# Layer 1's q and k by seven products over pairs of rows, normalised on ScalarE, with the order of four engines written out

## The chip, the cores and the metric

The kernel runs on one core of one Trainium2 chip. A core has five engines that run their own instruction queues and meet at semaphores: PE (TensorE, with a weight load, PEld, that overlaps the product before it), DVE (VectorE), ACT (ScalarE), POOL (GpSimd) and SP (SyncE, which here only issues DMAs). The metric is the device time of one execution in microseconds.

## The reference

`x` is 128 rows of 256 tokens with 256 channels. Two layers of attention follow, each with a group norm ahead of it and its input added back. All is float32.

```python
x = x + L0(gn(x))        # gated attention in each row, 8 heads of 32, a bias added after softmax
x = x + L1(gn(x))        # banded attention in each row, 4 heads of 64

def L1(x):                                   # x2: (128 rows, 256 tokens, 256 channels)
    q, k, v = split(x2 @ w_in.T + b_in, 3)
    scores = q @ k.T / sqrt(64), -inf where |i - j| > 16
    return softmax(scores) @ v @ w_out.T + b_out
```

The group norm of a layer needs the mean and variance over all rows, so layer 1 starts when layer 0 has ended. The bias of k adds the same number to all scores of one query, which softmax takes out again.

## The kernel before, and where the change touches it

A row is kept as [128 partitions, 2 halves, 256 tokens], channels on the partitions. A product of a [128x128] weight quarter with [128x256] of a row is two PE instructions, since the data are float32; a projection of 256 to 256 channels is four such products a row.

Layer 0 (lines 552 to 817) already computes its q, k, v and gate by seven products for eight. Two rows and two halves form a 2x2 block matrix `x[:, 0..3]`; POOL makes four sums of them (`sum_rows`, L584 to L587, tile `ts`), `sum_weights` (L158) has made the sums of the weight quarters once, `Seven.product` (L604) issues the seven products into a PSUM bank and a shared one, `Seven.take` (L619) copies what stands in the bank to SBUF on ACT between products, and `Seven.add` (L629) adds the copies together on POOL. `stretch` (L749) interleaves two weights (q with k, v with gate) and, between the late products, the four output products of an earlier row. In layer 0 the order of PE, ACT and DVE is the program's order (`manual_schedule`, L786).

Layer 1 (L826 on) has no such order: the tile framework's scheduler places its instructions. Its loop takes two rows a turn. For each row:

- `piece(s, 0)` (L836) normalises a row on DVE (`normalized`, L493: subtract the mean, multiply by rstd, two instructions of 128x256), and loads a pair of rows ahead (`load1`, L548, on SP).
- `piece(s, 1)` and `piece(s, 2)` make q and k by `by_channel` (L513, four products each) and copy them to SBUF on ACT, adding the bias (L849, two instructions each).
- `piece(s, 3)` makes v by 32 small products (L857) and copies it on ACT (L864).
- `scores` (L867) makes the band of the scores in blocks of 64 keys (L878), takes the exponential on ACT (L886), multiplies by the mask on POOL (`1p`, L888) and folds two halves together on POOL (`1zp`, L895).
- `attend` (L898) makes the weighted sum (L910) and the softmax's denominator (L920) in one pair of PSUM banks.
- `divide` (L927) copies the denominator on ACT (`1z`, L933), inverts it on DVE (`1rz`, L935), multiplies on DVE (`1at`, L937) and keeps its least value (`zmin`, L939).
- `project` (L941) is the output projection (four products, `1po`, L513), and `finish` (L945) adds bias and input (`1ot`, L956), transposes back (L960), both on DVE, and SP stores.

PSUM has eight banks. In layer 1 four are a ring (`psum(lay, "1", 4, 0)`, L827) that the scores, the projections and v all draw from in the order of issue; the other four are two pairs for `attend`.

A turn of the loop, for the rows s and s+1, issues: scores of s, s+1; attend of s-2, s-1; project of s-4, s-3; q and k of s+2, s+3; v of s+2, s+3; normalising of s+4, s+5; finish of s-4, s-3; divide of s-2, s-1.

Of the kernel before, what the change touches and what calls it, by code (L numbers as in the profile page):

```python
# [9 lines left out]
F32 = mybir.dt.float32  # L10
# [29 lines left out]
def conv_preact_kernel(  # L40
# [112 lines left out]
    sums = {w: const.tile([P, len(NS), P], F32, name=f"sums_{w}") for w in "qkvg"}  # L153

    def quarter(w, kt, m):
        source, col = (gate_sb, 0) if w == "g" else (qkv_sb, "qkv".index(w) * C)
        return source[:, kt, col + m * P : col + (m + 1) * P]

    def sum_weights():
        for w in "qkvg":  # L160
            s1, s2, s3, s4, n11 = (sums[w][:, n, :] for n in range(len(NS)))
            w00, w10, w01, w11 = (quarter(w, kt, m) for m in range(2) for kt in range(2))
            nc.gpsimd.tensor_tensor(s1, w01, w11, ALU.add)
            nc.gpsimd.tensor_tensor(s2, s1, w00, ALU.subtract)
            nc.gpsimd.tensor_tensor(s3, w00, w01, ALU.subtract)
            nc.gpsimd.tensor_tensor(s4, w10, s2, ALU.subtract)
            nc.gpsimd.tensor_scalar(n11, w11, -1.0, None, op0=ALU.mult)

    def stationary(w, n):

        if n <= 2:
            return quarter(w, n - 1, 0)
        return sums[w][:, NS.index({3: "s4", 4: "n11", 5: "s1", 6: "s2", 7: "s3"}[n]), :]
# [164 lines left out]
    with ExitStack() as early:  # L338
# [121 lines left out]
        for m in range(NM):  # L460
# [17 lines left out]
            if m == NM // 4:  # L478
                load_weights()
                sum_weights()  # L480
# [48 lines left out]

    x1 = dram.tile([S, 2, P, R], F32, name="x1")  # L530
# [8 lines left out]
    with ExitStack() as both:  # L539
        st1 = both.enter_context(tc.tile_pool(name="st1", bufs=1))  # L540
        stats1 = st1.tile([P, 2, S // 2, 6], F32, name="stats1")
        big1 = both.enter_context(tc.tile_pool(name="big1", bufs=2))
# [8 lines left out]
        with ExitStack() as lay0:  # L551
# [27 lines left out]
            def sum_rows(i):  # L579

                if 2 * i >= S:
                    return
                x, t = xns[i], row.tile([P, 4, R], F32, tag="ts", name=f"ts{i}", bufs=1)
                nc.gpsimd.tensor_tensor(t[:, 0], x[:, 2], x[:, 0], ALU.subtract)  # L584
                nc.gpsimd.tensor_tensor(t[:, 1], x[:, 3], t[:, 0], ALU.subtract)
                nc.gpsimd.tensor_tensor(t[:, 2], x[:, 3], x[:, 2], ALU.subtract)
                nc.gpsimd.tensor_tensor(t[:, 3], t[:, 1], x[:, 1], ALU.subtract)  # L587
                tss[i] = t

            class Seven:  # L590


                def __init__(self, w, i):
                    self.w, self.i = w, i
                    self.to = row.tile([P, 4, R], F32, tag=w, name=f"{w}{i}")
                    res[w, i] = self.to
                    self.mid = row.tile([P, 2, R], F32, tag="mid", name=f"mid{w}{i}")

                def open(self):
                    self.ps = proj_bank(f"p{self.w}{self.i}")  # L600

                def product(self, n, two=None):
                    x, t = xns[self.i], tss[self.i]
                    moving = {1: x[:, 0], 2: x[:, 1], 3: x[:, 3], 4: t[:, 3], 5: t[:, 0], 6: t[:, 1], 7: t[:, 2]}[n]  # L604
                    out = two if n == 2 else self.ps[:, 1 if n in (3, 5) else 0, :]

                    first = n == 1 or (n == 2 and self.w in "qv")
                    flags = dict(stop=n in (2, 3, 4), skip_group_check=True)
                    if self.w != "v":
                        nc.tensor.matmul(out, lhsT=stationary(self.w, n), rhs=moving, start=first, **flags)  # L610
                        return
                    for t2 in range(2):
                        cols = slice(t2 * P, (t2 + 1) * P)
                        nc.tensor.matmul(  # L614
                            out[:, cols], lhsT=moving[:, cols], rhs=stationary(self.w, n),
                            start=first and t2 == 0, **flags
                        )

                def take(self, what):  # L619
                    if what == "15":  # L620
                        nc.scalar.copy(self.to[:, 0:4:3, :], self.ps)
                    elif what == "6":
                        nc.scalar.copy(self.mid[:, 0, :], self.ps[:, 0, :])
                    elif what == "7":
                        nc.scalar.copy(self.mid[:, 1, :], self.ps[:, 0, :])
                    else:
                        nc.scalar.copy(self.to[:, 1:3, :], self.ps)

                def add(self, two):  # L629
                    nc.gpsimd.tensor_tensor(self.to[:, 0], self.to[:, 0], two, ALU.add)  # L630
                    nc.gpsimd.tensor_tensor(self.to[:, 2:4], self.to[:, 2:4], self.mid, ALU.add)
# [57 lines left out]
            def divide(s, zs):  # L689
# [3 lines left out]
                z = att.tile([P, 2, R], F32, tag="z", name=f"z{s}")  # L693
# [10 lines left out]
            def attend(s):  # L704
# [9 lines left out]
                at = row.tile([P, 2, R], F32, tag="at", name=f"at{s}")  # L714
# [20 lines left out]
            def output(s):  # L735

                if s < 0:
                    return
                st[s]["po"] = proj_bank(f"po{s}")
                for m in range(2):  # L740
                    for kt in range(2):
                        nc.tensor.matmul(  # L742
                            st[s]["po"][:, m, :], lhsT=out_sb[:, kt, m * P : (m + 1) * P],
                            rhs=st[s]["at"][:, kt, :],
                            start=(kt == 0), stop=(kt == 1),
                        )
                        yield

            def stretch(names, i, s):  # L749

                po = output(s)
                if 2 * i >= S:
                    for _ in po:
                        pass
                    return
                f, g = (Seven(w, i) for w in names)


                for p in (f, g):
                    p.open()  # L760
                    p.product(1)
                    p.product(5)
                    p.take("15")
                twos = proj_bank(f"p2{names}{i}")
                two = row.tile([P, 2, R], F32, tag="two", name=f"two{names}{i}")
                f.product(2, twos[:, 0, :])
                g.product(2, twos[:, 1, :])
                nc.scalar.copy(two, twos)  # L768
                for p in (f, g):
                    p.product(3)  # L770
                    p.product(6)
                    p.take("6")

                for n, what in ((7, "7"), (4, "34")):
                    f.product(n)
                    f.take(what)
                    next(po, None)
                    g.product(n)
                    g.take(what)
                for _ in po:  # L780
                    pass
                for n, p in enumerate((f, g)):
                    p.add(two[:, n, :])


            with tc.manual_schedule(engines={mybir.EngineType.PE, mybir.EngineType.Activation, mybir.EngineType.DVE}):  # L786
# [8 lines left out]
                for s in range(S + 1):  # L795
# [14 lines left out]
                    least(s - 1, z)  # L810
                    if s == S - 1:
                        most1 = join_most(st1, stats1, 1)
                        load1(0)
                        load1(1)
# [11 lines left out]
        with ExitStack() as lay:  # L826
# [3 lines left out]
            st, hd, outs = {}, {}, {}  # L830

            weights = [att.tile([P, 2, 2 * WROW], F32, name=f"1p{i}", bufs=1) for i in range(4)]
            for p in weights:
                nc.gpsimd.memset(p, 0.0)

            def piece(s, n):  # L836
                if s >= S:
                    return
                if n == 0:
                    if s % XG == 0:  # L840
                        load1(s // XG + 1)
                    st[s] = {"xn": normalized(row, ygs[s // XG][:, s % XG], mean1, rstd1, f"1_{s}")}
                elif n in (1, 2):
                    w = "qk"[n - 1]
                    ps = by_channel(w_in_t, (n - 1) * C, st[s]["xn"], f"p1{w}{s}")
                    a = row.tile([P, 2, R], F32, tag=w, name=f"1{w}{s}")
                    for half in range(2):
                        b = bqk[:, 2 * (n - 1) + half : 2 * (n - 1) + half + 1]
                        nc.scalar.activation(a[:, half, :], ps[:, half, :], AF.Identity, bias=b)  # L849
                    st[s][w] = a  # L850
                else:
                    xn = st[s]["xn"]
                    ps = proj_bank(f"p1v{s}").rearrange("p a (b c) -> p (a b) c", c=P)
                    for b in range(NB):
                        for kt in range(2):
                            for half in range(2):
                                nc.tensor.matmul(  # L857
# [335 lines left out]
```

## Time and profile before

| | us |
|---|---|
| median of 3 runs (2 of them 3288.93 and 3289.75) | 3289.35 |
| the profiled execution | 3289.14 |
| its span, first to last instruction | 3287.4 |
| PE busy | 3204.8 (97%) |
| DVE busy | 2732.7 (83%) |
| ACT busy | 1820.0 (55%) |
| POOL busy | 1250.6 (38%) |

The costliest groups that belong to layer 1, from the page's list: the reciprocal of the denominator on DVE (L935, 128 x 3342 ns), the products of q and k and of the output projection on PE (L513, 1024 instructions each at about 380 ns, pipelined), v's products (L857), the mask on POOL (L888, 128 x 1822 ns), the copies of q on ACT (L849, 256 x 470 ns), and the normalising on DVE (L493, 256 x 410 ns). A group's line gives: line, engine, operation, output and inputs, sizes, count, busy us, mean ns of one, and the idle time of the engine ahead of it with what ended that. A line of the order of time gives: start us, length us, engine, line, operation, tiles, count, and in brackets the engine's idle time just before and what ended it. Several instructions of one kind that follow each other are merged into one line.

### The profile page before, as it was taken

What the parts mean: (1) busy time and instruction counts of PE and PEld (TensorE: products, weight loads), DVE (VectorE), ACT (ScalarE), POOL (GpSimd) and SP (SyncE); (2) the same over time, 40 slices, a digit from 0 to 9 for tenths busy, and PEclk for the clock granted to TensorE, in tenths of its full rate; (3) what the DMA queues carried; (4) which work ended last, traced back from release to release, by engine and by line L of the source; (5) the groups of instructions that cost most, each with busy time, mean ns of one, the idle gap of its engine ahead of it and who ended that gap; (6) DMA issues with size and microseconds to landing.
All of it is one profiled execution on the core that took longest, in us unless ns stands there. A gap on an engine that the chain in (4) does not pass through costs nothing.

```text
span 3287.4 us, 86502 instructions
## 1 busy us (share of the span) xinstructions
PE 3204.8 (97%) x37193; PEld 2506.1 (76%) x37193; DVE 2732.7 (83%) x3794; ACT 1820.0 (55%) x3866; POOL 1250.6 (38%) x1135
## 2 busy tenths in 40 slices
PE   7799999999999999999999999799999999999997
PEld 4567777777777777777777777588888888888886
DVE  4759999999999999999999999667777777777776
ACT  4566666666666666666666666344444444444442
POOL 3034444444444444444444444133333323333232
PEclk8899999999999999999999999899999999999998
DMA  9931111111111111111111110012222222222221
GB/s 382 411 87 56 49 38 36 40 33 40 34 40 40 33 40 34 40 35 39 34 40 40 33 40 21 20 40 66 54 65 66 53 66 55 64 66 53 66 56 45
DMA packets 346327, 209.35 MB, mean 64 GB/s; under 512 B 273608, under 2 KB 339152, under 8 KB 339664
## 3 DMA queue, kind: packets, MB, share of 16 engines
q1 hardware_dynamic: 345040, 201.37, 21.2%
q8 instruction: 294, 4.82, 0.6%
q0 software_dynamic: 752, 2.36, 0.2%
q14 instruction: 97, 0.79, 0.1%
q10 hardware_dynamic: 144, 0.00, 0.0%
HBM read 136.59 MB, written 67.11 MB: 62 GB/s over the span
## 4 chain that ended last, share of the span: by engine, by line
PE 93%; DMA 3%; DVE 3%; ACT 0%; issue 0%; SPq 0%; DVEq 0%; ACTq 0%
PE sim L640 8%; PE p1v L857 7%; PE av L667 7%; PE 1po L513 7%; PE po L742 7%; PE p1q L513 7%; PE p1k L513 7%; PE bv L667 7%; PE pv L614 6%; PE pq L610 5%; PE pk L610 5%; PE pg L610 5%; PE zs L681 4%; DMA xs<-in_x_dram 3%; PE 1sim L878 3%; PE 1avz L910 2%
## 5 line engine op out<-in xcount | busy, mean ns | idle before, releaser
L651 ACT ACTIVATE ex<-sim 128x512 f32<-128x512 f32 x1024 | 527.4, 601 | 249.7 <-PE sim L640 249.7
L935 DVE RECIPROCAL 1rz<-1z 128x512 f32<-128x512 f32 x128 | 427.8, 3342 | 174.2 <-ACT 1z L933 174.2
L657 DVE TENSOR_TENSOR both<-ex 128x512 f32<-128x512 f32 x512 | 483.7, 984 | 77.8 <-ACT ex L651 77.8
L888 POOL TENSOR_TENSOR 1p<-1ex,seen 128x768 f32<-128x768 f32 x128 | 233.3, 1822 | 736.3 <-ACT 1ex L886 736.3
L697 DVE RECIPROCAL d<-d 128x512 f32<-128x512 f32 x128 | 429.2, 3353 | 4.4
L742 PE MATMUL po<-at,out_sb 128*128 128x256 f32 x1024 | 287.4, 384 | 12.1 <-DVE at L715 12.1
L849 ACT ACTIVATE 1q<-p1q,bqk 128x256 f32<-128x256 f32 x256 | 107.5, 470 | 345.1 <-PE p1q L513 345.1
L640 PE MATMUL sim<-q,k 32*128 32x256 f32 x4096 | 295.7, 401 | 1.1 <-ACT ex L651 1.1
L630 POOL TENSOR_TENSOR v<-v,twovg 128x256 f32<-128x256 f32 x64 | 72.8, 1137 | 551.1 <-ACT twovg L768 551.1
L640 PEld LDWEIGHTS sim<-q,k 32*128 32x128 f32 x4096 | 186.4, 184 | 102.7 <-issue 63.8
L513 PE MATMUL 1po<-1at,w_out_t 128*128 128x256 f32 x1024 | 242.7, 390 | 4.9 <-DVE 1at L937 4.9
L667 PE MATMUL av<-ex,v 128*32 128x256 f32 x4096 | 247.5, 382 | 0.0
L513 PE MATMUL p1q<-xn,w_in_t 128*128 128x256 f32 x1024 | 244.0, 381 | 2.0 <-DVE xn L493 1.1
L667 PE MATMUL bv<-bias_sb,v 128*32 128x256 f32 x4096 | 244.4, 379 | 0.0
L513 PE MATMUL p1k<-xn,w_in_t 128*128 128x256 f32 x1024 | 241.9, 379 | 0.0
L857 PEld LDWEIGHTS p1v<-w_in_t,xn 128*64 128x64 f32 x4096 | 222.2, 137 | 21.6 <-issue 21.6
L857 PE MATMUL p1v<-w_in_t,xn 128*64 128x128 f32 x4096 | 237.9, 274 | 0.0
L513 PEld LDWEIGHTS 1po<-1at,w_out_t 128*128 128x128 f32 x1024 | 191.6, 192 | 55.0 <-ACT 1z L933 23.9
L513 PEld LDWEIGHTS p1q<-xn,w_in_t 128*128 128x128 f32 x1024 | 195.3, 191 | 29.4 <-issue 1.3
L513 PEld LDWEIGHTS p1k<-xn,w_in_t 128*128 128x128 f32 x1024 | 194.7, 190 | 26.5
L742 PEld LDWEIGHTS po<-at,out_sb 128*128 128x128 f32 x1024 | 187.0, 193 | 34.1 <-issue 7.7
L493 DVE TENSOR_SCALAR xn<-yg,mean,rstd 128x256 f32<-128x256 f32 x256 | 93.9, 410 | 138.9 <-PE p1v L857 138.9
(226 smaller groups left out, 6708.1 us busy)
## 6 DMA issues: line engine op xcount, KB each, us to landing
pr<-in_L_conv_pair_repr_dram SPq DMA_DIRECT2D x32, 1024.0 KB, 23.0
x<-o SPq DMA_DIRECT2D x64, 512.0 KB, 2.8
yg<-x SPq DMA_DIRECT2D x64, 512.0 KB, 4.2
out_dram<-1o SPq DMA_DIRECT2D x256, 128.0 KB, 4.0
xg<-in_x_dram SPq DMA_DIRECT2D x252, 128.0 KB, 3.1
xs<-in_x_dram SPq DMA_DIRECT2D x15, 2048.0 KB, 21.7
xs<-in_x_dram SPq DMA_DIRECT2D x2, 1024.0 KB, 17.9
qkv_sb<-in_L_conv_qkv_proj_dram POOLq DMA_DIRECT2D x4, 192.0 KB, 12.6
```

Of the source, the lines that this page charges most:

```text
L513: nc.tensor.matmul(ps[:, m, :], lhsT=w[:, kt, col + m * P : col + (m + 1) * P], rhs=xn[:, kt, :], start=(kt == 0), stop=(kt == 1),)
L610: nc.tensor.matmul(out, lhsT=stationary(self.w, n), rhs=moving, start=first, **flags)
L614: nc.tensor.matmul(out[:, cols], lhsT=moving[:, cols], rhs=stationary(self.w, n), start=first and t2 == 0, **flags)
L640: nc.tensor.matmul(sims[j][:, kt, :], lhsT=k[p0 : p0 + D0, 2 * r + half, kt * P : (kt + 1) * P], rhs=q[p0 : p0 + D0, 2 * r + half, :], sta ...
L651: nc.scalar.activation(ex[:, j], sims[j], AF.Exp, scale=1.0 / math.sqrt(D0))
L657: nc.vector.tensor_tensor(both[:, j : j + 2], ex[:, j : j + 2, 0, :], ex[:, j : j + 2, 1, :], ALU.add)
L667: nc.tensor.matmul(to[D0 * j : D0 * (j + 1), half, :], lhsT=v[:, 2 * r + half, c0 : c0 + D0], rhs=weights(4 * half + j, kt), start=(kt == ...
L697: nc.vector.reciprocal(d, d)
L742: nc.tensor.matmul(st[s]["po"][:, m, :], lhsT=out_sb[:, kt, m * P : (m + 1) * P], rhs=st[s]["at"][:, kt, :], start=(kt == 0), stop=(kt == 1),)
L857: nc.tensor.matmul(ps[KB * half : KB * (half + 1), b, :], lhsT=xn[:, kt, KB * b : KB * (b + 1)], rhs=w_in_t[:, kt, 2 * C + P * half : 2 * ...
L888: nc.gpsimd.tensor_tensor(p.rearrange("p j (r c) -> p (j r) c", c=WROW)[:, :, 0 : 2 * WSTEP] .rearrange("p r (t c) -> p r t c", c=WSTEP)[: ...
L935: nc.vector.reciprocal(rz, z)
```

## The change

The helpers of layer 0 (`Quarters`, `row_sums`, `Seven`, `sevens`, and `one_by_one` for the output products) are lifted out so that both layers use them; layer 0 calls them in the order it had. In layer 0 the tiles `z` and `at` now have one buffer instead of two. The weight sums of layer 1's q and k are made in a new tile for each, by ten small POOL instructions.

Layer 1 is rewritten:

- `normal(i, by_scalar)` normalises a pair of rows in four instructions, the first two pairs on DVE, all others on ACT (`Identity` with scale and bias), and makes the four row sums on POOL.
- `stretch(i, po)` makes q and k of a pair by seven products each. q's bias goes in with three of ACT's copies; k's bias is left out. The four output products of one row stand between the late products.
- `divide` is split into `total`, `inverse`, `divide` and `least`, so that each can be placed.
- PE, ACT, DVE and POOL follow the order of the program.

```diff
+    class Seven:
+        def __init__(self, pool, weights, x, t, name, tag, by_token=False, bias=None):
...
+        def copy(self, to, ps, half):
+            if self.bias is None:
+                nc.scalar.copy(to, ps)
+            else:
+                nc.scalar.activation(to, ps, AF.Identity, bias=self.bias[:, half : half + 1])
+
+        def take(self, what):
+            if what == "15":
+                nc.scalar.copy(self.to[:, 0:4:3, :], self.ps)
+            elif what == "6":
+                self.copy(self.mid[:, 0, :], self.ps[:, 0, :], 0)
+            elif what == "7":
+                self.copy(self.mid[:, 1, :], self.ps[:, 0, :], 1)
+            elif self.bias is None:
+                nc.scalar.copy(self.to[:, 1:3, :], self.ps)
+            else:
+                self.copy(self.to[:, 1, :], self.ps[:, 0, :], 1)
+                nc.scalar.copy(self.to[:, 2, :], self.ps[:, 1, :])
+
+        def add(self, two):
+            nc.gpsimd.tensor_tensor(self.to[:, 0], self.to[:, 0], two, ALU.add)
+            nc.gpsimd.tensor_tensor(self.to[:, 2:4], self.to[:, 2:4], self.mid, ALU.add)
+
+    def sevens(pool, f, g, name, po):
+        for p in (f, g):
+            p.open()
+            p.product(1)
+            p.product(5)
+            p.take("15")
...
+        f.product(2, twos[:, 0, :], first=True)
+        g.product(2, twos[:, 1, :])
+        if f.bias is None:
+            nc.scalar.copy(two, twos)
+        else:
+            f.copy(two[:, 0, :], twos[:, 0, :], 0)
+            g.copy(two[:, 1, :], twos[:, 1, :], 0)
+        for p in (f, g):
+            p.product(3)
+            p.product(6)
+            p.take("6")
+        for n, what in ((7, "7"), (4, "34")):
+            f.product(n)
+            f.take(what)
+            next(po, None)
+            g.product(n)
+            g.take(what)
+        for _ in po:
+            pass
+        for n, p in enumerate((f, g)):
+            p.add(two[:, n, :])
...
-                z = att.tile([P, 2, R], F32, tag="z", name=f"z{s}")
+                z = att.tile([P, 2, R], F32, tag="z", name=f"z{s}", bufs=1)
...
+                        if by_scalar:
+                            nc.scalar.activation(x, y, AF.Identity, bias=shift1[:, col], scale=rstd1[:, col])
+                        else:
+                            nc.vector.tensor_scalar(
+                                x, y, mean1[:, col], rstd1[:, col], op0=ALU.subtract, op1=ALU.mult
+                            )
+                tss[i] = row.tile([P, 4, R], F32, tag="ts", name=f"1ts{i}", bufs=2)
+                row_sums(tss[i], xns[i])
...
+            with tc.manual_schedule(engines={
+                mybir.EngineType.PE, mybir.EngineType.Activation, mybir.EngineType.DVE, mybir.EngineType.Pool
+            }):
+                normal(0, False)
+                values(0)
+                values(1)
+                normal(1, False)
+                nc.vector.scalar_tensor_tensor(shift1, mean1, -1.0, rstd1, op0=ALU.mult, op1=ALU.mult)
+                stretch(0, iter(()))
+                for s in range(0, S + 4, 2):
+                    if s < S:
+                        scores(s)
+                        scores(s + 1)
+                    one, two = (s - 2, s - 1) if s <= S else (-1, -1)
+                    attend(one)
+                    attend(two)
+                    total(one)
+                    total(two)
+                    for _ in project(s - 4):
+                        pass
+                    inverse(one)
+                    finish(s - 4)
+                    divide(one)
+                    inverse(two)
+                    divide(two)
+                    least(one)
+                    least(two)
+                    stretch(s // 2 + 1, project(s - 3))
+                    finish(s - 3)
+                    normal(s // 2 + 2, True)
+                    values(s + 2)
+                    values(s + 3)
```

## The prediction

> **What bounds the kernel now.** I read the slices of the span first, then the chain that ended last, then busy time by stretch, then the order of time inside one turn of layer 1's loop.
>
> ```profile
> PE   7799999999999999999999999799999999999997
> DVE  4759999999999999999999999667777777777776
> ACT  4566666666666666666666666344444444444442
> POOL 3034444444444444444444444133333323333232
> PE 93%; DMA 3%; DVE 3%; ACT 0%; issue 0%; SPq 0%; DVEq 0%; ACTq 0%
> 2360.00:3240.00 880.00, 880.00 (x12571) 777.59 (x12570) 652.33 (x890) 371.49 (x886) 303.05 (x198) 1.00 0.24 60
> ```
>
> The dip of PE in the slices, near 2100 us, parts layer 0 from layer 1. In the last row (PE, PEld, DVE, ACT, POOL, clock) PE works in all of 880 us of layer 1 at full clock, DVE in 74%, ACT in 42%, POOL in 34%. So a product removed from PE is time gained, as long as nothing else comes late. One turn (two rows) in weight loads of PE:
>
> ```profile
> 2799.98 1.37 PEld L878 LDWEIGHTS 1sim<-1q,1k 64*64 64x64 f32 x61 [0.17 <-issue]
> 2803.63 3.32 PEld L513 LDWEIGHTS 1po<-1at,w_out_t 128*128 128x128 f32 x16 [0.39 <-ACT 1z L933]
> 2806.97 1.70 PEld L513 LDWEIGHTS p1q<-xn,w_in_t 128*128 128x128 f32 x8
> 2808.70 1.70 PEld L513 LDWEIGHTS p1k<-xn,w_in_t 128*128 128x128 f32 x8
> 2814.19 3.47 PEld L857 LDWEIGHTS p1v<-w_in_t,xn 128*64 128x64 f32 x64 [0.33 <-issue]
> 2817.83 1.37 PEld L878 LDWEIGHTS 1sim<-1q,1k 64*64 64x64 f32 x61 [0.17 <-issue]
> ```
>
> A turn is 2817.83 - 2799.98 = 17.85 us. From 2157.45 (the scores of rows 4 and 5, the first turn with everything in it) to 3246.19 (the last scores) there are 61 of them. From q to k is 1.73 us for four products of 128x256 (eight instructions, two to an f32 product): 0.4325 us a product.
>
> **What goes.** q and k take 16 products a turn before and 14 after: 2 x 0.4325 = 0.865 us less on PE, which nothing covers. The 32 small products of v, the scores, the attention and the eight output products stay, at their prices.
>
> **What is added, and where it lies.** Layer 0 already runs this scheme, so most rows are at hand. Times below count from a turn's first scores.
>
> *PE waits for ACT inside the stretch.* Products 6, 7 and 4 of one weight go to one bank in turn, and each must first be copied out. Layer 0 shows how tight this is:
>
> ```profile
> 1015.30 0.41 PEld L610 LDWEIGHTS pq<-ts,sums_q 128*128 128x128 f32 x2
> 1016.14 0.37 ACT L623 COPY midq<-pq 128x256 f32<-128x256 f32 x1 [0.27 <-PE pq L610]
> 1016.59 0.41 PEld L610 LDWEIGHTS pq<-ts,sums_q 128*128 128x128 f32 x2
> ```
>
> The copy begins 0.84 us after product 6's load and ends at 1016.51; product 7 loads 0.08 later. Other weight loads go 0.05 us after the copy that they wait for, so 0.03 us is spare. In layer 1 q's copies add a bias. The row for that is L849 (below), 0.470 us, not 0.373. Two round trips of q (6 to 7, 7 to 4) come 0.07 us late each: **+0.14 us** a turn. If the copies were no longer it is 0; if all four round trips, k's too, stalled by the full 0.1 it is 0.4. k's copies carry no bias and have an output product between, so I keep 0.14.
>
> *POOL.* It gets eight instructions a turn: four row sums and two adds (256 and 512 wide) for each of q and k. The scores of the next turn wait for the last add.
>
> ```profile
> L630 POOL TENSOR_TENSOR q<-q,twoqk 128x256 f32<-128x256 f32 x54 | 40.5, 750 | 253.8 <-ACT twoqk L768 253.8
> L630 POOL TENSOR_TENSOR k<-k,twoqk 128x256 f32<-128x256 f32 x54 | 63.3, 1172 | 0.0
> L631 POOL TENSOR_TENSOR q<-q,midq 128x512 f32<-128x512 f32 x55 | 70.0, 1272 | 86.3 <-ACT q L627 86.3
> L631 POOL TENSOR_TENSOR g<-g,midg 128x512 f32<-128x512 f32 x54 | 92.6, 1714 | 0.0
> L849 ACT ACTIVATE 1q<-p1q,bqk 128x256 f32<-128x256 f32 x256 | 107.5, 470 | 345.1 <-PE p1q L513 345.1
> L493 DVE TENSOR_SCALAR xn<-yg,mean,rstd 128x256 f32<-128x256 f32 x256 | 93.9, 410 | 138.9 <-PE p1v L857 138.9
> ```
>
> The same instruction has two prices in layer 0: 0.75 or 1.17 us, 1.27 or 1.71. In the order of time the dear ones lie beside DVE sums of two SBUF tiles (both, d). The Trainium skill's page "SBUF — State Buffer", section "Who interferes with whom", says that a VectorE instruction with two SBUF inputs, or in a two-port mode, contends with GpSimd, and one with a single SBUF input does not. Layer 1's VectorE work after the change (reciprocal, reduce, transposes, and sums with one input in PSUM) is of the free kind, and before the change L895 on POOL takes 1.27 us beside zmin and ot there. So I take the cheap prices; the dear ones are the other end.
>
> Cheap: q's last output leaves ACT at about 12.6 (product 4 of q loads at 10.9, +0.84, then 0.47 + 0.37). POOL then does 1.27 + 0.72 + 1.27 and is done at 15.9; the scores come at 17.1: 1.2 us spare. The four row sums follow (2.8 us, to 18.7), just ahead of the next turn's mask product, which waits for its exponentials until 17.1 + 1.94 = 19.0. POOL's sum is 2 x (1.82 + 1.27) + 4.0 + 3.0 = 13.2 us of 17.1. Cost on the path: 0.
>
> *Normalising moves from DVE to ACT.* The page "ScalarE: Activation LUTs", "Rules for kernel authors", speaks against it: multiply and add belong on VectorE; with its 0.3 us + 0.83 ns an element I estimate 0.51 us for 256 elements, against 0.41 on DVE. The nearest row is L849's 0.470, at a pitch of 0.42. Four are 1.7 us by the row, 2.05 by the page. Either is hidden: ACT sums to about 11.3 us of 17.1 (exponentials 1.6, z 1.6, copies of q and k 5.1, this 1.8, v 1.2). They run from 13.2 to 15.0, and v's copy, queued behind them, is not due until about 15.4. With the page's 0.3 us more v's bank still comes free in time. DVE loses 1.6 us; 12.5 us remain.
>
> *The order by hand.* DVE does: reciprocal, output of row s-4, divide, reciprocal, divide, two reduces, output of row s-3. It starts at 3.5, when z is there. The first output product's bank is read by 8.2, wanted again at 10; the second is read by about 15, wanted at 17.5. SP's order is unchanged: a load of yg waits for the output of the same turn (15.4), takes its 4.2 us and is wanted ten later. Dropping k's bias adds no instruction.
>
> *Layer 0.* Its order on PE, DVE, ACT and SP stays. Tiles z and at get one buffer. z is written at 1008.73 and last read (zmin) by 1004.6; at is written at 1015.41 and last read at about 1005.7: covered by 4 us or more. Ten weight sums (0.45 us each in L163's rows, 4.4 us) stand on POOL ahead of layer 0's first row sum. POOL idles there from 185.7 to 193.99, so 0; 4.4 us once if they are released only at the end of that gap.
>
> *Start and end of layer 1.* Now: first xn at 2116.4, scores at 2129.75, 2143.05, 2157.45. After: v first, at PE's slow start, to 2122.4; q and k with no output products between, so their round trips show (0.07 + 0.33 + 0.17 + 0.23 = 0.8 us); then POOL's adds in the open. Scores at 2133.2 (+3.4); the next is 1.0 us shorter, since the 1.1 us wait for the activation table moves under POOL's adds; then 0.1 shorter. Net **+2.4 us**. The tail is a chain on DVE, ending 3279.05 now; laid out again it is **0.5 us** shorter.
>
> **Sum** against the profiled execution (3289.14 us, span 3287.4; the median of the runs is 3289.35, the same to 0.2 us): 61 x (0.865 - 0.14) = 44.2 off, +2.4, -0.5: 42.3 us off, **3247 us**.
>
> **Rivals.**
> - *No stalls at all* (layer 0's stretch shows none): 61 x 0.865 = 52.8, less 2: 3238. Chance 0.13.
> - *POOL's answer comes late but not every engine does.* At the dear prices the adds take 1.71 + 1.17 + 1.71 = 4.6 us and end at 17.25, some 0.2 us past the scores; with 0.2 more in round trips a turn costs 0.4 us: 61 x 0.325 = 20 off, and 2 for the start: 3267; milder forms lie between. For it: the rows of layer 0. Against: the pairing above. Chance 0.20.
> - *POOL becomes the bound, slower than before.* It decides once POOL's 13.2 us exceed 17.85, a stretch of 1.35. At dear prices for all twelve, with the mask and zp at 1.4 times, 4 x 1.18 + 2 x 1.17 + 2 x 1.71 + 8.65 = 19.1 us: 61 x 1.25 = 76 us more, 3366. Against it: 1.82 and 1.27 are steady beside DVE's reciprocals. Chance 0.05.
> - Several small waits eating all: no change, 0.03.
>
> The forecast has 0.59. What a measurement tells from no change here is 0.2%, 6.6 us. Faster 0.92, within 0.03, slower 0.05. The range takes in the first rival and most of the second: 3236 to 3266; the forecast's own range is 3241 to 3254.
>
> **What would show it.** Right: from scores to scores 17.1 us; PE still full in the stretch; midq at 0.47 us with a gap before product 7; POOL rows at 0.75 and 1.27; scores not waiting for POOL; new xn on ACT below 0.51. Wrong: POOL rows above 1 us for 256 elements, scores that wait for k's last add, an output product waiting for DVE, or layer 0 longer than 2116 us up to the first xn.

## The result, and the profile after

| | before | after |
|---|---|---|
| median of 4 runs, us | 3289.28 (3288.93 to 3289.75) | 3257.86 (3255.89 to 3260.11) |
| the profiled execution, us | 3289.14 | 3257.72 |
| its span, us | 3287.4 | 3256.0 |

The ratio is 0.9905, with a 95% interval of 0.9887 to 0.9922: 31.4 us are gone, where 42.3 were forecast. The time lies in the range of 3236 to 3266, though above the forecast's own 3241 to 3254: the regular turn is better than forecast, and nearly 20 us were lost in a place that the prediction doesn't speak of. The same slices of the page first, then the stretch of layer 1 (PE, PEld, DVE, ACT, POOL, clock, DMA share, GB/s), both of the kernel after:

```profile
PE   6799999999999999999999999799999999999997
DVE  4759999999999999999999999857777777776667
ACT  4566666666666666666666666466666666665663
POOL 3034444444444444444444444287777777776774
PE 92%; DMA 3%; DVE 3%; issue 1%; ACT 0%; POOL 0%; SPq 0%; DVEq 0%; ACTq 0%
2360.00:3210.00 850.00, 836.30 (x12308) 725.90 (x12305) 599.56 (x681) 539.34 (x1217) 627.31 (x586) 1.00 0.25 62
```

POOL goes from 34% of layer 1 to 74%, ACT from 42% to 63%, DVE falls a little. The new entry is small: the chain of waits has 1% of "issue", time in which PE waited for nothing that the profile shows, and PE works in 836.30 of 850 us where it had worked in all of 880.

One regular turn in weight loads of PE (only the rows that part it):

```profile
2830.36 0.41 PEld L565 LDWEIGHTS p1q<-1ts,sums_1q 128*128 128x128 f32 x2
2831.80 0.30 PEld L565 LDWEIGHTS p1q<-1ts,sums_1q 128*128 128x128 f32 x2 [0.17 <-issue]
2832.12 0.41 PEld L634 LDWEIGHTS 1po<-1at,w_out_t 128*128 128x128 f32 x2
2833.12 0.30 PEld L565 LDWEIGHTS p1q<-1ts,sums_1q 128*128 128x128 f32 x2 [0.17 <-issue]
2835.48 3.47 PEld L917 LDWEIGHTS p1v<-w_in_t,1xn 128*64 128x64 f32 x64 [0.33 <-issue]
2839.12 1.37 PEld L938 LDWEIGHTS 1sim<-1q,1k 64*64 64x64 f32 x61 [0.17 <-issue]
```

Products 6, 7 and 4 of q are the first, second and fourth rows. The scores before these went out at 2822.08, so this turn is 17.05 us: 0.80 less than before, of the 0.865 that two products cost. Times from scores to scores for all 61 turns, worked out from the start of each turn's first exponential, add up to 1088.7 us before (each 17.85) and 1059.4 after. 61 turns of 17.05 would be 1040.1. The missing 19.4 us lie in a few long turns; ten that follow each other near the end hold 18.1 of them (turn n takes the scores of rows 2n and 2n+1):

```
turn   48     49     50     51     52     53     54     55     56     57     58     59 ...
us   17.05  21.29  18.86  18.31  18.57  19.08  18.76  18.27  18.54  18.69  18.21  17.2-17.8
```

What happens in them is in the chain of waits of the kernel after, here for the first long turn (start us, us, what):

```profile
2960.70 0.39 PE 1avz L980 x5
2961.09 0.50 PE 1avz L970 x21
2961.59 2.24 issue
2963.83 0.39 PE 1avz L970 x9
2964.22 0.50 PE 1avz L980 x6
2964.72 3.41 PE 1po L634 x8
```

PE stops for 2.24 us in the midst of 64 products whose operands have been there for most of a turn. No engine is waited for. The other terms: the first exponential of turn 2 comes at 2157.96 (2158.45 before), and from the first exponential of the last turn to the end of the span are 38.6 us (40.2 before). So -48.7 + 19.4 - 0.5 - 1.6 = -31.4 us.

### The profile page after: what moved, and what is told of

Same layout as the page of the kernel before. It is cut to its first block, busy times and chain, and to the rows that moved or that the text cites. A ratio compares the mean times of both kernels' runs of the same rounds, so it can differ in the third digit from the quotient of the medians.

```text
span 3256.0 us, 86773 instructions
## 1 busy us (share of the span) xinstructions
PE 3151.5 (97%) x36937; PEld 2442.3 (75%) x36937; DVE 2678.8 (82%) x3547; ACT 2041.1 (63%) x4306; POOL 1683.4 (52%) x1657
## 4 chain that ended last, share of the span: by engine, by line
PE 92%; DMA 3%; DVE 3%; issue 1%; ACT 0%; POOL 0%; SPq 0%; DVEq 0%; ACTq 0%
PE sim L702 8%; PE p1v L917 7%; PE av L729 7%; PE 1po L634 7%; PE po L634 7%; PE bv L729 7%; PE pv L569 6%; PE pq L565 6%; PE p1q L565 5%; PE pk L565 5%; PE p1k L565 5%; PE pg L565 5%; PE zs L743 4%; DMA xs<-in_x_dram 3%; PE 1sim L938 3%; PE 1avz L970 2%
## 5 line engine op out<-in xcount | busy, mean ns | idle before, releaser
L592 POOL TENSOR_TENSOR v<-v,twovg 128x256 f32<-128x256 f32 x64 | 72.8, 1137 | 551.3 <-ACT twovg L608 551.3
L634 PE MATMUL 1po<-1at,w_out_t 128*128 128x256 f32 x1024 | 271.5, 389 | 5.0 <-DVE 1at L1004 3.1
L917 PEld LDWEIGHTS p1v<-w_in_t,1xn 128*64 128x64 f32 x4096 | 223.6, 137 | 22.0 <-issue 22.0
L917 PE MATMUL p1v<-w_in_t,1xn 128*64 128x128 f32 x4096 | 239.1, 275 | 1.1 <-DVE 1xn L883 1.1
L592 POOL TENSOR_TENSOR q<-q,twoqk 128x256 f32<-128x256 f32 x64 | 47.2, 737 | 298.5 <-ACT twoqk L608 298.5
L729 PEld LDWEIGHTS av<-ex,v 128*32 128x32 f32 x4096 | 120.1, 109 | 108.2 <-issue 42.1
L729 PEld LDWEIGHTS bv<-bias_sb,v 128*32 128x32 f32 x4096 | 133.1, 110 | 87.9
L684 DVE TENSOR_SCALAR xn<-xt,mean,rstd 128x256 f32<-128x256 f32 x256 | 196.8, 808 | 0.0
L593 POOL TENSOR_TENSOR 1q<-1q,mid1q 128x512 f32<-128x512 f32 x64 | 81.6, 1274 | 191.2 <-ACT 1q L589 191.2
L955 POOL TENSOR_TENSOR 1zp<-1p 128x512 f32<-128x512 f32 x128 | 162.6, 1270 | 10.0
```

The source lines that it names most:

```text
L634: nc.tensor.matmul(ps[:, m, :], lhsT=w[:, kt, m * P : (m + 1) * P], rhs=at[:, kt, :], start=(kt == 0), stop=(kt == 1),)
L684: nc.vector.tensor_scalar(xns[i][:, 2 * r + half, :], xt[:, half, :], mean0[:, half : half + 1], rstd0[:, half : half + 1], op0=ALU.subtra ...
L729: nc.tensor.matmul(to[D0 * j : D0 * (j + 1), half, :], lhsT=v[:, 2 * r + half, c0 : c0 + D0], rhs=weights(4 * half + j, kt), start=(kt == ...
L917: nc.tensor.matmul(ps[KB * half : KB * (half + 1), b, :], lhsT=xns[i][:, 2 * r + kt, KB * b : KB * (b + 1)], rhs=w_in_t[:, kt, 2 * C + P * ...
```

## The experiments

**What could stop PE.** The list of DMA queues has one queue with this many packets of instructions, MB and share of the DMA engines' time:

```profile
q8 instruction: 292, 4.78, 0.6%
```

Each of them is 16384 bytes. The trace of this kernel holds 74,426 instructions of PE (weight loads, products and waits at semaphores), 255 for each packet, so I take a packet for a block of 256. Counted from 0 in the order of the trace, there are eleven places in the turns of layer 1 where more than 0.8 us pass from one PE instruction to the next, and at each of them the number of the next instruction leaves 193 when it is divided by 256: the border of a block. A turn has 508 such instructions, four fewer than two blocks, so the border moves by four from turn to turn. PE issues the 288 weight loads and products of scores and attention, all small, in the first 3.7 us of a turn and the rest in 13.4 us. The DMA traffic around a turn's first scores (columns as above; the first row of before, the second of after):

```profile
2817.00:2821.60 4.60, 4.60 (x163) 4.04 (x159) 0.99 (x3) 2.92 (x7) 1.82 (x1) 1.00 0.02 4
```

```profile
2820.50:2825.10 4.60, 4.60 (x166) 4.43 (x164) 0.45 (x2) 2.99 (x7) 4.20 (x6) 1.00 0.58 170
```

Before, the 16 DMA engines are idle there (2%), after, 58% busy: the load of `yg` and the four stores of a pair of rows, which before ran ten us behind the scores beside large products. Theory: the packet with PE's next block is held up behind that burst, and when a whole block falls into the 288 quick instructions, PE runs dry. The kernel before fits it: its turn has 514 instructions, so its borders move by two a turn and walk over the same places (turns 4 to 27), and without a burst there PE stops nowhere. Rival: something that belongs to the time or place in the program, whatever the blocks. Four ways to tell:

**e1_phase.** 80 more PE instructions once, early, to move the borders:

```diff
-            nc.tensor.transpose(pb[:, 0:8], b_raw, ident[0:8, 0:8])
+            for _ in range(41):
+                nc.tensor.transpose(pb[:, 0:8], b_raw, ident[0:8, 0:8])
```

> The changed kernel with one tiny transpose of the early stage (the 8x8 bias turn in turn_weights) done 41 times in place of once: 80 more PE instructions ahead of layer 1, about 4 us of PE beside the stage that waits for DMA. Nothing else is moved. Theory I (PE runs out of instructions: its code comes in blocks of 256 instructions, a turn has 508, so the place of a block's edge in the turn moves by 4 each turn; the stretch from 195 down to 155, which the changed kernel met in turns 49 to 59, is where a fetch that waits behind the turn's loads and stores comes too late): the edge now passes that stretch in turns 5 to 15. The long turns (18 to 21 us) move there, turns 49 to 59 become 17.05 us, the total stays near 3258 us. Theory C (something tied to the time of the run or to the late part of the program: clock, heat, memory): turns 49 to 59 stay long.

Measured: 3264.34 us (3252.97 to 3270.25), too scattered for the total to say much. Its turns say it: turns 5 to 17 are now long (21.31, 18.01, 18.85, 18.85, 18.80 ...), those near 49 are 17.05, and the loss is 19.5 us again, with eleven such places, each before a number that leaves 193. That is where the count puts it: 80 instructions are 20 steps of four, 49 + 20 = 69, and the borders come round after 64 turns, so 5. The loss moved by 44 turns without any change to layer 1's code.

**e2_nostore.** The stores of layer 1 left out:

```diff
-                    for a in range(A):
-                        nc.sync.dma_start(out=in_strips(out[0], s - 1, 2, a), in_=o[strip(a)])
+                    if s == S - 1:
+                        for a in range(A):
+                            nc.sync.dma_start(out=in_strips(out[0], s - 1, 2, a), in_=o[strip(a)])
```

> The changed kernel without the stores of the output, all but those of the last two rows (the output is left undone otherwise; each turn still loads its rows). Theory I with the stores as what delays the fetch: fetches no longer wait past the turn's border, no turn is longer than 17.1 us, 61 turns are 19 us shorter, total about 3238 us. If the load of the next rows (512 KB at the same place) is enough to delay the fetch, the long turns stay, perhaps shorter (17.5 to 18.5 us), total 3245 to 3255. Theory C: unchanged, 3258.

Measured: 3247.22 us (3244.06 to 3247.93). Turns 49 to 57 are still long, but 17.4 to 18.8: 6.5 us lost in place of 19.4. The stores made two thirds of it, the load the rest.

**e3_late_store.** The stores kept, but of each pair the odd row's transposes and the stores go out 7.5 to 9.0 us into the next turn:

```diff
                     inverse(one)
+                    store(s - 5)
                     finish(s - 4)
```

> The changed kernel with the transposes of a pair's second row, and so the pair's stores, put off to the next turn, behind the first reciprocal: the stores go out some 7 us after the scores begin, while PE does q and k, where 256 instructions last over 12 us. All work is kept. Theory I: the fetches come in time, turns are 17.05 us (17.3 at most, DVE has 0.9 us more ahead of the output row), total 3238 to 3243 us, and this version beats both. Theory C: 3258.

Measured: 3247.23 us (3246.89 to 3247.56), with 6.2 us lost in turns 49 to 58. Moving the stores is worth what leaving them out is: not their bytes cost time, but where they lie.

**e4_512.** One tiny product more, so that a turn has 512 PE instructions and the borders stand still:

```diff
+                if s >= 6 and r == 0:
+                    nc.tensor.matmul(
+                        ps[0:KB, 0, 0:2], lhsT=xns[i][:, 0, 0:KB], rhs=w_in_t[:, 0, 2 * C : 2 * C + 2],
+                        start=True, stop=True,
+                    )
```

> The changed kernel with one more tiny product (64x2, four PE instructions) ahead of v in each turn from the third on, overwritten by v's first: a turn has then 512 PE instructions, two blocks of 256, and the edge of a block stays where it is in the turn (at 119, a place where the changed kernel had 17.05 us). Theory I: no long turns, each turn about 0.1 us longer for the product (17.15), total about 3244 us. Theory C: 3258 and 6 more, 3264.

Measured: 3246.39 us (3245.89 to 3248.54). No long turn is left, with the burst where it was; each turn is 17.16, since the product itself costs 0.115 (7.0 us in 61 turns).

**e5_late_both.** Built on e3: the load of `yg` is called behind `store(s - 5)`.

> Instruction starvation theory (PE's instruction blocks are held up by the burst of stores and load at the turn's border): the store and the load of yg are both moved some 9 us behind the border, so no turn should be long for any place of the block borders. 61 turns of 17.05 us, against 1059.4 measured in the changed kernel: 19.4 us less, so 3238 us (3236 to 3241). If the load by itself, wherever it stands, or the 508 instructions of a turn made the long turns, they stay and the time is about 3247, as with the late store alone.

Measured: 3246.81 us (3244.57 to 3249.81), 6.3 us lost: a miss. SP's queue of this run shows that the edit didn't move what it was to move (start us, us, engine, line, operation):

```profile
2822.60 0.40 SPq L659 DMA_DIRECT2D yg<-x  x1
2831.40 2.02 SPq L1049 DMA_DIRECT2D out_dram<-1o  x4
```

The load still goes out ahead of the stores, at the turn's border: SP is not among the engines whose order follows the program, and the framework placed it. So e5 is e3 again.

**e7_order_on_sp.** e5 with `mybir.EngineType.SP` added to the engines of `manual_schedule`.

> e5_late_both once more, but with SP's order written out too: in e5 the load of yg was placed ahead of the stores and still went out 0.5 us behind the turn's first scores, so the burst of the load stayed at the border. Now load and stores both go out some 9 to 11 us behind it. Starvation theory: no long turns at all, 61 turns of 17.05 us, 3238 us (3235 to 3241). If what remained in e3_late_store and e5_late_both (8 us in turns 49 to 57) did not come from the load at the border, it stays: 3246.

Measured: 3240.77 us (3235.77 to 3242.34), ratio 0.9848 [0.9835, 0.9862]. No turn is over 17.14 us; 61 turns take 1040.0 us. In the profiled execution (3241.64 us) the first exponential is at 2133.5 in place of 2130.9; what comes ahead of the turns, not the turns, holds most of what the total is above the expectation. The traffic at the border, and later in the turn, in this kernel:

```profile
2822.00:2826.60 4.60, 4.60 (x143) 4.43 (x143) 1.30 (x3) 3.47 (x8) 4.19 (x7) 1.00 0.02 4
2826.60:2831.20 4.60, 4.60 (x77) 3.88 (x70) 3.05 (x1) 2.08 (x7) 4.52 (x3) 1.00 0.01 4
2831.20:2836.00 4.80, 4.80 (x23) 4.01 (x22) 4.73 (x9) 3.24 (x8) 2.33 (x3) 1.00 0.52 121
```

The same bytes now move beside the large products. The packets of PE's instructions show the step itself. Turns 49 and 50 have the same instructions and borders in both kernels (worked out from the packets of the instruction queue; us from the turn's first scores):

```
             after: packet goes out, PE stands      e7: packet goes out, PE stands
turn 49            +2.96              2.24                 +0.08              0 (turn of 17.14 us)
turn 50            +2.42              1.58                 +0.02              0
```

With the burst at the border the packet leaves 2.4 to 2.9 us later, and PE goes on some 1.4 us after the packet's end. It doesn't wait for the whole burst: in turn 49 the burst's last packet ends at +6.0. This kernel is the fastest that leaves nothing out: 17 us below the changed one.

**e6_worst_lock.** The counter-test: e4's 512 instructions, with the borders locked where they hurt, by 48 more instructions once (`range(25)` in e1's line).

> As e4_512 (512 PE instructions a turn), but with 48 more PE instructions once, early on, so that every turn starts at index 175 of a block of 256 instructions in place of 127. Starvation theory: index 151 to 187 gave turns of 18.2 to 18.9 us when it was passed through, so now nearly all of 61 turns are that long: 61 x (18.6 - 17.16) = 88 us more than e4_512, about 3335 us (3310 to 3350), slower than the kernel before the change. If the place of the borders is not the cause, the 48 instructions cost nothing and it is e4_512 again, 3246 to 3250.

Measured: 3340.63 us (3337.63 to 3341.62), ratio 1.0154 [1.0137, 1.017]. 59 of 61 turns are long (18.0 to 19.2, the first 21.1), 91.8 us over 61 x 17.16. Each of the 59 has one place where over 0.8 us pass between two PE instructions, and always the next one's number leaves 193 when divided by 256. The waits of this kernel, 2300 to 3200 us (us in total, times, longest):

```profile
ACT 1z L998 <- issue: 87.2, 48, 2.3
PEld 1avz L986 <- issue: 67.9, 48, 1.9
PE 1avz L986 <- issue: 59.9, 48, 1.7
```

48 instructions out of some 74,000, without effect on any data, turn a gain of 44 us (e4) into a loss of 51. The rival is out. That the packet is held by the burst is shown by moving the burst; how the queues share the DMA engines is not seen in these traces.

**e8_eight_in_order.** Which part of the change is the gain? On e7: q and k by eight products again, in the new order.

```diff
+                for s in (2 * i, 2 * i + 1):
+                    for n, w in enumerate("qk"):
+                        ps = by_channel(w_in_t, n * C, xns[i][:, 2 * (s % 2) : 2 * (s % 2) + 2], f"p1{w}{s}")
...
+                            nc.scalar.activation(a[:, half, :], ps[:, half, :], AF.Identity, bias=b)
```

> e7_order_on_sp with q and k by eight products again (16 a turn, both biases back, no row sums and no adds on POOL), all in the order written out for the engines, normalising on ScalarE. Theory (the products removed are the gain, the order by hand is worth nothing in a regular turn): a turn is 17.05 + 0.865 - 0.065 = 17.85 us, as before the change, and the time 3238 + 61 x 0.80 = 3287 us. Rival (the order itself saves time on PE): a turn below 17.6 us. Other rival (an order by hand costs time, and the saving is larger than it seems): above 18.1.

Measured: 3287.82 us (3283.35 to 3290.84), ratio 0.9996 [0.9989, 1.0002]; every turn is 17.85. The order by hand, ACT's normalising and the later stores give nothing by themselves: the removed products are all of the gain.

**e9_normal_on_dve.** On e7: `normal(s // 2 + 2, False)`, all normalising on DVE.

> e7_order_on_sp with all normalising on VectorE. Theory (hidden on either engine): DVE has 12.5 + 1.64 = 14.1 us a turn and 3 us of room at its end; xn comes 2.3 us later, POOL's row sums end some 3 us behind the scores in place of 1.6, which only takes from POOL's idle time. A turn stays 17.05 us, no time gained or lost: within 2 us of e7_order_on_sp. Rival (DVE needed the relief, or POOL's lateness reaches the scores): a turn longer by 0.3 us or more, 18 us in all.

Measured: 3241.07 us (3240.47 to 3243.63), turns of 17.05 but for a few up to 17.34 (0.4 us in all). It is hidden on either engine.

**e10_no_q_bias.** On e7: `bias=None` for q too.

> e7_order_on_sp without q's bias (left out of the computation), so that q's copies between the products take 0.37 us in place of 0.47. Prediction's stall of 0.14 us a turn: the turn falls by 0.14 to 16.91, 8.5 us in all. What the trace shows (the weight load is 0.14 us late twice, but it stands 0.11 us ahead of its product, so 0.03 us each reach the products): it falls by 0.065 to 16.985, 4 us in all. If PE isn't held there, nothing changes.

Measured: 3233.68 us (3231.57 to 3235.61); a turn is 16.985, 0.06 less, 3.9 us in all; the rest of the difference to e7 lies ahead of the turns and in the scatter. In this run the weights of product 7 go out 0.48 us behind the load before them, near the pitch of 0.43:

```profile
2828.95 0.41 PEld L565 LDWEIGHTS p1k<-1ts,sums_1k 128*128 128x128 f32 x2
2829.43 0.37 PEld L565 LDWEIGHTS p1q<-1ts,sums_1q 128*128 128x128 f32 x2
2829.82 0.41 PEld L634 LDWEIGHTS 1po<-1at,w_out_t 128*128 128x128 f32 x2
```

From product 7's load to the next is 0.39 us here, 0.87 for both steps. In the changed kernel product 7's load comes 0.57 us behind the one before it, held for 0.14, but the next one follows 0.32 later, 0.89 for both, so 0.03 of each delay is left.

## Why the prediction was right, and where not

- **PE is the bound, and a product removed is time gained**: right. 0.865 was the size of what goes: a turn of e8, with eight products, is 17.85 us, and one of e10, with seven and without q's longer copies, 16.985: 0.865 apart.
- **The stall of 0.14 us a turn**: the mechanism is right (q's copies take 0.474 us, and the weight loads of products 7 and 4 show a gap), the size is not: 0.06, shown by e10. The step counted how late the weight load is as how late the product is. A load in this stretch stands 0.21 us ahead of its product (2831.23 and 2831.44); product 7's, 0.14 late, still stands 0.07 ahead (2831.80 and 2831.87), and what is lost is 0.03. With it the 61 turns give 48.7 us rather than 44.2.
- **POOL at the cheap prices**: right. The rival at the dear prices needed 1.17 and 1.71; here are the rows (2300 to 2950 us), with q's copy and the normalising below:

```profile
L593 POOL TENSOR_TENSOR 1q<-1q,mid1q 128x512 f32<-128x512 f32 x38 | 48.4, 1274 | 116.0 <-ACT 1q L589 116.0
L592 POOL TENSOR_TENSOR 1k<-1k,two1qk 128x256 f32<-128x256 f32 x38 | 27.9, 735 | 0.0
L576 ACT ACTIVATE mid1q<-p1q,bqk 128x256 f32<-128x256 f32 x76 | 36.1, 474 | 6.2
L881 ACT ACTIVATE 1xn<-yg,shift,rstd 128x256 f32<-128x256 f32 x152 | 78.8, 592 | 0.0
```

  The rule of the Trainium skill's page "SBUF — State Buffer" ("Who interferes with whom") that the prediction took its choice from agrees with these rows: beside VectorE work with at most one SBUF tile as input POOL's adds take 0.735 and 1.274 us. k's last add ends 1.2 us ahead of the scores (2837.88 against 2839.12), as forecast. The rival's own sum has a slip: its start costs 2 us, as in the forecast, so 20 off and 2 on are 3271, not 3267, and the range takes in less of it than the prediction says.
- **Normalising on ACT**: 0.592 us a piece, above the row (0.470), above the estimate from the page "ScalarE: Activation LUTs" (0.51) and so against the sign "below 0.51". That page's formula is stated for a bias per partition alone, and here the scale is one per partition too; no run parts the two. Four take 2.07 us at a pitch of 0.5. It is hidden, as forecast, and e9 shows that it would have been on DVE too.
- **The start of layer 1**: forecast +2.4, and -0.5 came. 1.25 us of that belong to layer 0, whose end wanders by some us between executions. From the first `xn` on, the first exponential is 0.35 us later than before (15.70 against 15.36) and the two turns after it together 0.41 longer, so +0.8. The step that failed let the first scores wait for k's last add. The adds of row s write `to[:, 0]` alone; the last add makes the next row. PE's first scores go out at 2129.91, behind `1k` L592 (2129.14 + 0.72) and while L593 (2129.82 + 1.27) still runs.
- **The tail**: 1.6 us shorter in place of 0.5.
- **"SP's order is unchanged"** is the step that cost the most: 19.4 us. It asked of the load only whether its data come in time, and of the stores nothing, so what the burst does to PE stood at 0 without a reason. But what they wait for had moved: before, DVE made both rows' outputs together, and the last `1ot` of the turn ended 9.6 us behind its scores (2809.61, scores at 2799.98); after, `finish(s - 3)` stands behind the stretch, and the last `1ot` ends at 2820.50, 1.6 us ahead of the next turn's scores. That frees the `yg` buffer and completes the stores' tile, so the burst of 1 MB slid from the large products to the small ones. The prediction says that the load is released at 15.4 and takes 4.2 us, which is 2.5 us past the border of a turn of 17.1. It didn't ask what else PE fetches there.
- **The sum**: -42.3 - 4.5 (stall) - 2.9 (start) - 1.1 (tail) + 19.4 (starvation) = -31.4 us. That 3257.86 lies so near to 3247 owes something to luck, errors that cancel; without the starvation the kernel is at 3240.77, below the forecast's own range and near the rival without stalls.

## What to carry to other kernels

When an edit moves the release of a DMA, ask not only whether its data come in time, but which instructions run while it moves: short ones use up a block of instructions in a few microseconds, and here the packet with the next block came late while the burst moved. A long stop of PE for "issue" at one instruction number modulo 256, in turns that come and go slowly, is its sign; a turn whose instruction count is just off a multiple of 256 walks through the good and the bad places. And a weight load that is late is not yet a late product.

## What was not expected of the hardware

- The Trainium skill's page "Runtime: NRT & Kernel Launch", section "Instruction fetch mechanics", says that an engine's instructions come in blocks of 256 through a DMA queue of its own, and that crossing a border is mostly hidden. The blocks are as it says (292 packets of 16384 bytes). Hidden they are in the kernel before and in e7, where PE stops at none; beside a burst of 1 MB PE paused for 0.8 to 2.5 us at a border, and e6 lost 92 us.
- Behind the longest of these stops the clock was down too. Behind it, and behind the next long turn's stop, PE's clock was granted so in the changed kernel (the seventh column of numbers, after POOL's):

```profile
2963.80:2968.20 4.40, 4.37 (x27) 3.33 (x27) 1.54 (x2) 0.69 (x2) 2.79 (x2) 0.64 0.03 6
2984.50:2989.00 4.50, 4.50 (x34) 3.68 (x34) 3.80 (x6) 1.31 (x4) 3.39 (x3) 1.00 0.02 5
```

  After 2.24 us of standing still the eight instructions of the output projection took 3.48 us, after 1.58 us they took 1.99; the turns lost 4.2 and 1.8 us. The first stops of e1 and e6, 1.97 us each, show the same, 0.65 and 0.63. The length of a stop doesn't decide it alone: ahead of the first scores PE waited 2.31 us for POOL in the changed kernel and in e7, and behind that the clock was 1.00 in the one and 0.65 in the other. What decides it stays open.
